# Biases kept in the weights' first row, put there on chip, in place of bias matmuls

## The chip, the cores and the metric

The kernel runs on one core of a Trainium2 chip. A core has five engines that run their own instruction queues and wait for one another by semaphores: PE (TensorE, matmuls; PEld is its weight load), DVE (VectorE), ACT (ScalarE), POOL (GpSimd) and SP (SyncE, which here only issues DMAs). The DMA transfers of all queues run on 16 DMA engines. The metric is the device time of one execution in microseconds, as the median of the runs.

## The reference

One transformer layer over x of 4 x 1024 x 512 in float32: a layernorm, an attention with 16 heads of 128, and a product in rounded fp8 values, added to x.

```python
xn = _layernorm(x)                                  # no scale, no shift
q  = apply_rope(rmsnorm(xn @ Wq + bq, qn_w))        # 16 heads x 128
lk = apply_rope(rmsnorm(xn @ Wlk + blk, kn_w))
lv = xn @ Wlv + blv
w_cmp   = softmax(xn @ Wcmp + bcmp) over each 4 rows
entries = weighted sum of each 4 rows of xn
ck = apply_rope(rmsnorm(entries @ Wk + bk, kn_w));  cv = entries @ Wv + bv
ctx_sparse = softmax over the 8 best (q . ck, causal) @ cv
ctx_local  = softmax over the window of this and the last 128 rows (q . lk) @ lv
out = x + 0.5 * (ctx_sparse + ctx_local) @ Wo + bo + fp8(xn * scale) @ fp8(input2 * scale1) / (scale * scale1)
```

A row of xn has mean zero: its 512 features add up to 0.

## The kernel before

**Tiling.** The 4096 rows are 32 chunks t of 128 rows (8 chunks c of each of 4 batches). The 16 heads are 8 units u of 2 heads, so there are 256 units n = 8t + u. The weights of all units stay in SBUF: wqk_sb[u] (128 x 4 x 512: the columns of Wq and Wlk for the two heads, 4 slices of 128 input features), wlv_sb[u] (128 x 4 x 256) and wo_sb[u].

**Order.** The program is written out by hand in the loop at L789, one step s for each unit, in a software pipeline; each engine runs its instructions in this order. In step s, PE does the scores of unit s (L570 to L581), the queries and keys of unit s + 2 (L443, then a bias matmul L444), the output product of unit s - 2 (L751), the values of unit s + 1 (L535) and the context of unit s - 1 (L718). DVE and ACT do the softmaxes of unit s (weigh, settle, settle_window), then turn (L659) the probabilities of unit s, then normalize and rotate q and lk of unit s + 2 (L465, L308 to L310), with GpSimd for 1/sqrt (L288, L289) and part of the rotation (L307).

**The way through DRAM.** From unit 8 on (by_dma), transposed operands are made in two parts: DVE transposes blocks of 32 x 32 (L659 for the probabilities, L510 and L513 for q and lk), and the blocks change places by a DMA to DRAM and another back. All of them are on SP's queue, in this order in a step: pr out (L667), four probT in (L701), four qk out (L518), qT and lkT in (L528). SP stops at each until the transfer before has landed or the tile is ready. lkT of unit s + 2, made at the end of step s, is read by the scores of that unit (L577).

**Biases.** bq and blk are added by L444: a selection column of sel, spread over 128 columns, times bias_b, which holds the biases split in three bf16 parts (small_constants, L196 to L201). blv is added after the softmax, where the weights of a row add up to 1: keep_context (L733) adds blvT with the factor 0.5, one instruction for each head.

**Work of a chunk.** chunk_prep(t) is a generator, advanced by steps() twice in each step; it begins at u = 7 two chunks ahead and makes layernorm (L327 to L335), the transposed xnT (L340, L343), and the compressed entries. chunk_eight(t), begun at u = 3, rounds xnT to fp8 values (quantize: three DVE passes, four GpSimd passes) and multiplies them with w2_sb (L423). x8 has one buffer. Weights come in by DMA in the first steps: units 0 to 2 on SP's queue, the others on ACT's in steps -2 to 6.

Of the kernel before, what the change touches and what calls it, by code (L numbers as in the profile page):

```python
# [12 lines left out]
F32 = mybir.dt.float32  # L13
BF16 = mybir.dt.bfloat16
U32 = mybir.dt.uint32
AF = mybir.ActivationFunctionType
# [3 lines left out]
P = 128  # L20
# [18 lines left out]
def kernel(  # L39
# [109 lines left out]
    with nc.allow_non_contiguous_dma(reason="512 words once"):  # L149
        nc.scalar.dma_start(  # L150
            wkv_sb[:, :, 2 * D : 2 * D + 1], Wcmp.rearrange("(k p) o -> p k o", p=P)
        )
    bias_f = work.tile([P, 1024], F32, tag="probT", name="bias_f", bufs=1)[0:BLK, 0:512]
    nc.vector.memset(bias_f, 0.0)
    nc.scalar.dma_start(bias_f[0:NU, 0:256], bq.rearrange("(u n) -> u n", u=NU))
    nc.scalar.dma_start(bias_f[0:NU, 256:512], blk.rearrange("(u n) -> u n", u=NU))
    bkv_sb = const.tile([NE, 2 * D], F32, name="bkv_sb")
    nc.scalar.dma_start(bkv_sb[:, 0:D], bk.partition_broadcast(NE))
    nc.scalar.dma_start(bkv_sb[:, D : 2 * D], bv.partition_broadcast(NE))
    norm_w = const.tile([P, 2, D], F32, name="norm_w")  # L160
    nc.scalar.dma_start(norm_w[:, 0, :], qn_w.partition_broadcast(P))
    nc.scalar.dma_start(norm_w[:, 1, :], kn_w.partition_broadcast(P))
    blv_n = work.tile([P, 2, P], F32, tag="cT", name="blv_n", bufs=1)[0:NH, 0, :]
    nc.scalar.dma_start(blv_n, blv.rearrange("(h d) -> h d", h=NH))
    bcmp_sb = const.tile([P, 1], F32, name="bcmp_sb")
    nc.scalar.dma_start(bcmp_sb, bcmp.partition_broadcast(P))
    scales = const.tile([P, 2], F32, name="scales")
# [11 lines left out]
    make_identity(nc, ident)  # L179
    ident_b = const.tile([P, P], BF16, name="ident_b")  # L180
    inv = const.tile([P, 1], F32, name="inv")
    bias_b = const.tile([P, 512], BF16, name="bias_b")
    nc.vector.memset(bias_b, 0.0)
    sel = const.tile([P, NU], BF16, name="sel")
    mask_b = const.tile([P, 2 * P + NE], BF16, name="mask_b")
    bo_sb = const.tile([P, HID], F32, name="bo_sb")
    blvT = const.tile([P, NH], F32, name="blvT")

    def small_constants():
        nc.vector.tensor_scalar(  # L190
            norm_w[:, 0, :], norm_w[:, 0, :], 1.0 / math.sqrt(D), None, ALU.mult
        )

        part = work.tile([P, 1024], F32, tag="probB", name="part", bufs=1).bitcast(BF16)
        part = part[0:BLK, 0:512]
        nc.vector.tensor_copy(bias_b[0:BLK, :], bias_f)  # L196
        nc.vector.tensor_tensor(bias_f, bias_f, bias_b[0:BLK, :], ALU.subtract)
        nc.vector.tensor_copy(part, bias_f)
        nc.vector.tensor_copy(bias_b[BLK : 2 * BLK, :], part)
        nc.vector.tensor_tensor(bias_f, bias_f, part, ALU.subtract)  # L200
        nc.vector.tensor_copy(bias_b[2 * BLK : 3 * BLK, :], bias_f)  # L201

        nc.vector.tensor_tensor(
            sel, ident[:, 0:NU], ident[:, BLK : BLK + NU], ALU.add
        )
        nc.vector.tensor_tensor(
            sel, sel, ident[:, 2 * BLK : 2 * BLK + NU], ALU.add
        )
# [36 lines left out]
    def late_constants():  # L245

        nc.scalar.dma_start(bo_sb, bo.partition_broadcast(P))
        nc.vector.tensor_tensor(inv, scales[:, 0:1], scales[:, 1:2], ALU.mult)
        nc.vector.reciprocal(inv, inv)

        bp = pp("blvT_ps")
        nc.tensor.transpose(bp[:, 0:NH], blv_n, ident[:NH, :NH])
        nc.scalar.activation(blvT, bp[:, 0:NH], AF.Copy, scale=0.5)

    def quantize(dst, src, scalar, tag):

        v = scratch(f"qv_{tag}") if tag[0] == "x" else src
        m = scratch(f"qm_{tag}")  # L260
        nc.vector.tensor_scalar(v, src, scalar, None, ALU.mult)
        nc.vector.tensor_scalar(
            m.bitcast(U32), v.bitcast(U32), 0x7F800000, None, ALU.bitwise_and
        )
        nc.vector.tensor_scalar(m, m, FP8_MIN_NORMAL, 1.5 * 2.0**20, ALU.max, ALU.mult)
        nc.gpsimd.tensor_tensor(v, v, m, ALU.add)
        yield
        nc.gpsimd.tensor_tensor(v, v, m, ALU.subtract)
        yield
        nc.gpsimd.tensor_scalar(m, v, FP8_OVERFLOW, 0.0, ALU.mult, ALU.mult)  # L270
        yield
        nc.gpsimd.tensor_tensor(dst, v, m, ALU.add)
        yield
# [5 lines left out]

    def round_w2():  # L280
        for k in range(KK):
            yield from quantize(w2_sb[:, k, :], w2_raw[k], scales[:, 1:2], f"w2_{k}")

    def rstd_of(ss, n, mul, eps, name):

# [30 lines left out]
    def chunk_prep(t):  # L316
# [14 lines left out]
        if c == 0:  # L331
            nc.gpsimd.memset(cv, 0.0)
        yield "B0"
        xn = scratch(f"xn_{t}")
        nc.vector.tensor_scalar(xn, xt, st[:, 6:7], r, ALU.subtract, ALU.mult)  # L335
        yield "A1"
        yield "B1"
        xp = pp(f"xp_{t}")
# [10 lines left out]
        for k in range(KK):  # L349
# [21 lines left out]
        )  # L371
        nc.scalar.activation(row[:, 0, :], row[:, 0, :], AF.Exp)
        yield "B3"
        yield "A4"
        spread_w = work.tile([P, NE], F32, tag="spread", name=f"spread_{t}", bufs=1)
        nc.vector.transpose(row[:, 1, :], row[:, 0, :])
        nc.vector.tensor_scalar(spread_w, picks, row[:, 1, 0:1], None, ALU.mult)
        yield "B4"
        ep = pp(f"ep_{t}")
        nc.tensor.matmul(ep[0:NE, 0 : 2 * D + 1], spread_w, y, start=True, stop=True)  # L380
        yield "A5"
        total = work.tile([NE, 1], F32, tag="total", name=f"total_{t}", bufs=1)
        kv = work.tile([NE, 2, D], F32, tag="kv", name=f"kv_{t}", bufs=1)
# [6 lines left out]
            ALU.mult,  # L390
            ALU.add,
        )
        yield "B5"
        g, o = divmod(c * NE, P)
        nc.scalar.copy(cv[o : o + NE, g, :], kv[:, 1, :])
# [16 lines left out]
        nc.vector.tensor_copy(ckT[:, ts(c, NE)], cp[:, 0:NE])  # L412
        yield "B8"

    def chunk_eight(t):

        xt, xnT = x_tiles["sum", t], chunks[t]
        x8 = work.tile([P, KK * P], BF16, tag="x8", name=f"x8_{t}", bufs=1)
        src = xnT.rearrange("p k s -> p (k s)")
        yield from quantize(x8, src, scales[:, 0:1], f"x_{t}")  # L420
        fp = pp(f"fp_{t}")
        for k in range(KK):
            nc.tensor.matmul(  # L423
                fp, x8[:, ts(k, P)], w2_sb[:, k, :], start=(k == 0), stop=(k == KK - 1)
            )
        yield
        f = scratch(f"f_{t}")
        nc.vector.scalar_tensor_tensor(f, fp, inv, bo_sb, ALU.mult, ALU.add)
        nc.gpsimd.tensor_tensor(xt, xt, f, ALU.add)
# [4 lines left out]
    def place(n):  # L434

        return divmod(n, NU)

    def queries(n):
        t, u = place(n)
        xnT = chunks[t]  # L440
        qp = psum.tile([P, 512], F32, tag="qp", name=f"qp_{n}")
        for k in range(KK):
            nc.tensor.matmul(qp, xnT[:, k, :], wqk_sb[u][:, k, :], start=(k == 0), stop=False)  # L443
        nc.tensor.matmul(  # L444
            qp, sel[:, u : u + 1].to_broadcast([P, P]), bias_b, start=False, stop=True
        )
        ss = work.tile([P, 4], F32, tag="ss", name=f"ss_{n}")
        units[n] = {"qp": qp, "ss": ss}

# [80 lines left out]
    def values_of(n):  # L530
        t, u = place(n)
        xnT = chunks[t]
        vp = pp(f"vp_{n}")
        for k in range(KK):
            nc.tensor.matmul(  # L535
                vp[:, 0:256],
                xnT[:, k, :],
                wlv_sb[u][:, k, :],
                start=(k == 0),
                stop=(k == KK - 1),  # L540
            )
        units[n]["vp"] = vp

    def keep_values(n):
# [180 lines left out]
        w["cp"] = cp  # L725

    def keep_context(n):
        _, u = place(n)
        w = units[n]
        cT = work.tile([P, 2, P], F32, tag="cT", name=f"cT_{n}", bufs=1)  # L730
        cp = w.pop("cp")
        for h in range(2):
            nc.scalar.activation(  # L733
                cT[:, h, :],
                cp[:, h, :],
                AF.Identity,
                bias=blvT[:, 2 * u + h : 2 * u + h + 1],
                scale=0.5,
            )
        w["cT"] = cT  # L740

    outs = {}
# [46 lines left out]
    for s in range(-2, NN + 2):  # L789
# [3 lines left out]
            running = [*running[-2:], chunk_prep(t + 2)]  # L793
        if u == 3 and 0 <= t < NT:
            load_x(t, "sum")
            running = [*running[-2:], chunk_eight(t)]
        if u == 4 and 0 <= t and t + 2 < NT:
            load_x(t + 2, "norm")
# [32 lines left out]
        if s + 2 >= NU:  # L831
            for_unit(s + 2, (turn_keys,), (fetch_keys,))
        for_unit(s + 1, (keep_values,))
        if s < NU:

            if s == -1:
                late_constants()
                for k in range(KK):
                    nc.scalar.dma_start(w2_raw[k], input2[ts(k, P), :])
            if 0 <= s < KK:  # L840
# [57 lines left out]
```

## Time and profile before

| | us |
|---|---|
| median of 3 runs | 2824.78 |
| lowest, highest | 2822.69, 2830.02 |
| profiled execution | 2828.88 |
| its span in the trace | 2827.2 |
| mean granted PE clock | 0.997 |

In the profile "busy" is the time in which an engine had an instruction running. The ends of matmuls are modelled, and they overlap, so what a matmul costs in a stream is read from the starts of two in a row. "us to landing" of a DMA runs from its issue. A line of the timeline gives start, duration, engine, line, operation and tiles.

```profile
POOL 3433222222233332232223233222223222322222
PEclk9999999999999999999999999999999999999999
HBM read 212.53 MB, written 184.03 MB: 140 GB/s over the span
```

The first two rows are 40 slices of the span, in tenths: POOL is busy 20 to 40% all along, and PE's clock is full throughout.

### The profile page before, as it was taken

How to read it: one execution, taken by the hardware profiler on the slowest of the kernel's cores; microseconds unless marked ns; L12 is line 12 of the kernel's file. 1: busy time of each engine (PE TensorE's matmuls, PEld its weight loads, DVE VectorE, ACT ScalarE, POOL GpSimd, SP SyncE). 2: the span in 40 equal slices, each digit the busy share in tenths (PEclk: the TensorE clock that was granted, in tenths of full speed). 3: DMA queues.
4: the chain of work that ended last, by engine and by line, in shares of the span. 5: the costliest groups of instructions: out<-in, count | busy, mean ns of one | idle time of the engine just before them, and what ended most of it. 6: DMA issues, size and time to landing. Idle time of an engine off the chain costs nothing. (4 is left out here: it accounts for less than half of the span.)

```text
span 2827.2 us, 48528 instructions
## 1 busy us (share of the span) xinstructions
PE 2775.0 (98%) x12770; PEld 1879.6 (66%) x12969; DVE 2277.4 (81%) x9132; ACT 1302.9 (46%) x5075; POOL 818.0 (29%) x1161
## 2 busy tenths in 40 slices
PE   7999999999999999999999999999999999999998
PEld 4666666666666666666666666666666666666666
DVE  5778888888777888888877788888887777888886
ACT  3444444444444444444444444444444444444443
POOL 3433222222233332232223233222223222322222
PEclk9999999999999999999999999999999999999999
DMA  7344445555444445555544444555554444455553
GB/s 224 93 140 133 137 143 151 147 153 146 133 128 133 138 134 149 148 152 151 148 129 123 137 134 138 150 153 147 149 146 124 134 131 131 136 152 151 149 149 116
DMA packets 620851, 399.85 MB, mean 141 GB/s; under 512 B 306880, under 2 KB 573984, under 8 KB 620576
## 3 DMA queue, kind: packets, MB, share of 16 engines
q1 hardware_dynamic: 608352, 383.18, 47.8%
q10 hardware_dynamic: 12224, 13.56, 1.5%
q8 instruction: 105, 1.72, 0.3%
q14 instruction: 170, 1.39, 0.2%
HBM read 212.53 MB, written 184.03 MB: 140 GB/s over the span
## 5 line engine op out<-in xcount | busy, mean ns | idle before, releaser
L443 PE MATMUL qp<-wqk,xnT 128*128 128x512 f32 x2048 | 944.6, 604 | 4.1 <-DMA scales<-in_L_ffn_scale_dram 3.1
L443 PEld LDWEIGHTS qp<-wqk,xnT 128*128 128x128 f32 x2048 | 370.1, 191 | 383.9 <-issue 370.3
L610 ACT ACTIVATE prob<-sc,neg 128x256 f32<-128x256 f32 (+1 forms) x512 | 236.1, 461 | 786.4 <-DVE taken L609 772.5
L535 PEld LDWEIGHTS vp<-wlv,xnT 128*128 128x128 f32 x2048 | 391.1, 191 | 170.4 <-issue 109.5
L535 PE MATMUL vp<-wlv,xnT 128*128 128x256 f32 x2048 | 488.6, 382 | 6.2 <-DVE lkT L495 2.9
L751 PE MATMUL op<-wo,cT 128*128 128x512 f32 x1024 | 488.0, 599 | 6.0 <-ACT cT L733 1.5
L659 DVE STREAM_TRANSPOSE probB<-prob 128x512 f32<-128x512 f32 (+2 forms) x494 | 282.9, 610 | 79.4 <-ACT prob L641 75.8
L294 ACT ACTIVATE junk<-qp 128x128 bf16<-128x128 f32 x1024 | 284.2, 278 | 100.0 <-remote 56.6
L307 POOL TENSOR_TENSOR rb<-th,cs 128x256 f32<-128x256 f32 x256 | 247.4, 966 | 276.5 <-DVE th L465 276.5
L465 DVE SCALAR_TENSOR_TENSOR th<-qp,r,norm_w 128x128 f32<-128x128 f32 x1024 | 282.9, 338 | 45.1 <-POOL r L289 44.9
L751 PEld LDWEIGHTS op<-wo,cT 128*128 128x128 f32 x1024 | 186.5, 190 | 179.2 <-issue 115.9
L547 ACT COPY lv<-vp 128x256 f32<-128x256 f32 x256 | 95.4, 373 | 449.5 <-PE cp L718 393.5
L288 POOL TENSOR_SCALAR r<-ss 128x4 f32<-128x4 f32 x256 | 49.8, 195 | 862.8 <-ACT junk L294 856.4
L718 PE MATMUL cp<-probT,lv 128*128 128x128 f32 x1920 | 298.3, 275 | 0.7 <-DMA probT<-pr 0.7
L718 PEld LDWEIGHTS cp<-probT,lv 128*128 128x128 f32 x1920 | 275.3, 192 | 14.3 <-PE vp L535 1.1
L289 POOL TENSOR_TENSOR r<-r,nhalf 128x4 f32<-128x4 f32 x256 | 259.9, 1015 | 21.4
L718 PE MATMUL cp<-probT,cv 128*128 128x128 f32 x1536 | 255.6, 275 | 0.0
L580 PE MATMUL sc<-ckT,qT 128*128 128x96 f32 (+7 forms) x1024 | 226.2, 303 | 0.0
L641 ACT ACTIVATE prob<-prob,tot 128x256 f32<-128x256 f32 (+1 forms) x512 | 223.0, 484 | 2.1 <-DVE tot L635 2.0
L309 DVE TENSOR_TENSOR th<-thb,rb 128x128 f32<-128x128 f32 x256 | 87.1, 340 | 158.9 <-POOL rb L307 158.9
L577 PE MATMUL sc<-lkT,qT 128*128 128x128 f32 x1024 | 209.7, 287 | 5.4 <-DMA lkT<-qk 3.9
L718 PEld LDWEIGHTS cp<-probT,cv 128*128 128x128 f32 x1536 | 213.2, 192 | 0.0
(123 smaller groups left out, 4003.8 us busy)
## 6 DMA issues: line engine op xcount, KB each, us to landing
pr<-probB SPq DMA_DIRECT2D x127, 512.0 KB, 2.6
probT<-pr SPq DMA_DIRECT2D x508, 128.0 KB, 2.9
qk<-thb SPq DMA_DIRECT2D x992, 64.0 KB, 2.0
pr<-probB SPq DMA_DIRECT2D x96, 384.0 KB, 2.3
probT<-pr SPq DMA_DIRECT2D x384, 96.0 KB, 2.5
qT<-qk SPq DMA_DIRECT2D x248, 128.0 KB, 2.3
lkT<-qk SPq DMA_DIRECT2D x248, 128.0 KB, 2.5
x_norm<-_attn_hidden_states_dram SPq DMA_DIRECT2D x32, 256.0 KB, 3.1
```

The costliest lines, as they stand in the source:

```text
L289: nc.gpsimd.tensor_tensor(r, r, nhalf[: ss.shape[0], 0:n], ALU.pow)
L294: nc.scalar.activation(junk[: src.shape[0]], src, AF.Square, accum_out=acc)
L307: nc.gpsimd.tensor_tensor(bb, x12, wide(cs[:, HALF:ROPE]), ALU.mult)
L443: nc.tensor.matmul(qp, xnT[:, k, :], wqk_sb[u][:, k, :], start=(k == 0), stop=False)
L465: nc.vector.scalar_tensor_tensor(th[:, i, :], qp[:, ts(i, D)], r[:, i : i + 1], norm_w[:, i // 2, :], ALU.mult, ALU.mult,)
L535: nc.tensor.matmul(vp[:, 0:256], xnT[:, k, :], wlv_sb[u][:, k, :], start=(k == 0), stop=(k == KK - 1),)
L580: nc.tensor.matmul(sc[:, spa], q, ckT[:, 0:m], start=True, stop=False)
L610: nc.scalar.activation(prob[:, loc], sc[:, loc], AF.Exp, bias=neg[:, 0:1], scale=-1.0, accum_out=tot[:, 0:1],)
L641: nc.scalar.mul(prob[:, loc], prob[:, loc], tot[:, 0:1])
L659: nc.vector.transpose(pb[:, :, ds(h * g, g), :], prob[:, parts[0] * P : (parts[-1] + 1) * P].rearrange("p (g b i) -> p b g i", b=NB, i=BLK),)
L718: nc.tensor.matmul(blocks(cp[:, h, :]), v, probT[:, :, h * len(parts) + i - parts[0], :], start=(i == parts[0]), stop=(i == parts[-1]),)
L751: nc.tensor.matmul(op, cT[:, h, :], wo_sb[u][:, h, :], start=(u == 0 and h == 0), stop=(u == NU - 1 and h == 1),)
```

## The change

In chunk 0 the biases are added as before by bias matmuls, and blv now likewise, on vp. From chunk 1 on no bias is added at all: xnT's first feature is set to 1.0 and the first row of the weights holds the bias. The feature that this displaces is had from the others: since the features of a row add up to zero, x0 = -(x1 + ... + x511), so the weights' first row w0 is subtracted from all rows, which makes w0 itself 0, and the bias is written in its place. The subtraction is done in SBUF by DMAs that accumulate into the weights (fold_first_row), two for each unit from POOL's queue in steps 3 to 10, from a DRAM row "less" that holds -w0 (first_rows, step -1). One step later put_biases writes the biases by three small DMAs from SP. For the sum to be zero to the last bits, layernorm gets a second centring pass. quantize of chunk t + 2 moves into chunk_prep, since it must read xnT before the first feature is set.

```diff
-    bias_f = work.tile([P, 1024], F32, tag="probT", name="bias_f", bufs=1)[0:BLK, 0:512]
+    bias_f = work.tile([P, 1024], F32, tag="probT", name="bias_f", bufs=1)[0:BLK, 0:768]
...
+    nc.scalar.dma_start(bias_f[0:NU, 512:768], blv.rearrange("(u n) -> u n", u=NU))
...
-    blv_n = work.tile([P, 2, P], F32, tag="cT", name="blv_n", bufs=1)[0:NH, 0, :]
-    nc.scalar.dma_start(blv_n, blv.rearrange("(h d) -> h d", h=NH))
...
-        bp = pp("blvT_ps")
-        nc.tensor.transpose(bp[:, 0:NH], blv_n, ident[:NH, :NH])
-        nc.scalar.activation(blvT, bp[:, 0:NH], AF.Copy, scale=0.5)
...
+    less = dram.tile([NU, 768], F32, name="less", bufs=1)
+
+    def first_rows():
+        row = work.tile([P, 1024], F32, tag="probT", name="first_rows", bufs=1)[0:NU, 0:768]
+        for i, w in enumerate((Wq, Wlk, Wlv)):
+            nc.sync.dma_start(row[:, ts(i, 256)], w[0].rearrange("(u n) -> u n", u=NU))
+        nc.gpsimd.tensor_scalar(row, row, -1.0, None, ALU.mult)
+        nc.gpsimd.dma_start(less, row)
+
+    def fold_first_row(u):
+        for w, cols in ((wqk_sb[u], ds(0, 512)), (wlv_sb[u], ds(512, 256))):
+            row = less[u, cols].partition_broadcast(P).unsqueeze(1)
+            nc.gpsimd.dma_start(w, row.to_broadcast([P, KK, w.shape[2]]), accum_op=ALU.add)
+
+    def put_biases(u):
+        for w, at, bias in ((wqk_sb[u], 0, bq), (wqk_sb[u], 256, blk), (wlv_sb[u], 0, blv)):
+            nc.sync.dma_start(w[0:1, 0, ds(at, 256)], bias[ts(u, 256)].partition_broadcast(1))
...
-        nc.vector.tensor_scalar(xn, xt, st[:, 6:7], r, ALU.subtract, ALU.mult)
+        off = work.tile([P, 1], F32, tag="off", name=f"off_{t}")
+        nc.vector.tensor_scalar(xn, xt, st[:, 6:7], 0.0, ALU.subtract, ALU.add, accum_out=off)
+        nc.vector.tensor_scalar(off, off, 1.0 / HID, None, ALU.mult)
+        nc.vector.tensor_scalar(xn, xn, off, r, ALU.subtract, ALU.mult)
...
         yield "B3"
+        if t:
+            eights[t], step = begin_eight(t)
+            next(step)
+            nc.vector.memset(xnT[0:1, 0, :], 1.0)
         yield "A4"
...
+    def begin_eight(t):
+        x8 = work.tile([P, KK * P], BF16, tag="x8", name=f"x8_{t}")
+        src = chunks[t].rearrange("p k s -> p (k s)")
+        return x8, quantize(x8, src, scales[:, 0:1], f"x_{t}")
...
+    def add_biases(out_, u, cols):
+        nc.tensor.matmul(
+            out_, sel[:, u : u + 1].to_broadcast([P, P]), bias_b[:, cols], start=False, stop=True
+        )
...
-        nc.tensor.matmul(
-            qp, sel[:, u : u + 1].to_broadcast([P, P]), bias_b, start=False, stop=True
-        )
+        if not t:
+            add_biases(qp, u, ds(0, 512))
...
+        if not t:
+            add_biases(vp[:, 0:256], u, ds(512, 256))
...
-        for h in range(2):
-            nc.scalar.activation(
-                cT[:, h, :],
-                cp[:, h, :],
-                AF.Identity,
-                bias=blvT[:, 2 * u + h : 2 * u + h + 1],
-                scale=0.5,
-            )
+        nc.scalar.activation(cT, w.pop("cp"), AF.Copy, scale=0.5)
...
+        if u == (5 if t else 4) and 0 <= t < NT:
             running = [*running[-2:], chunk_eight(t)]
...
         for_unit(s + 1, (keep_values,))
+
+        if 0 <= s - 3 < NU:
+            fold_first_row(s - 3)
+        if 0 <= s - 4 < NU:
+            put_biases(s - 4)
```

The other three steps of the moved quantize are advanced at the three next places of chunk_prep; chunk_eight then begins at u = 5 with the product. The scratch of quantize for the second weight comes from a part of wo_sb that is not loaded yet.

More of the change, by code (lines that the diff above doesn't have):

```diff
@@ L181 @@
     inv = const.tile([P, 1], F32, name="inv")
-    bias_b = const.tile([P, 512], BF16, name="bias_b")
+    bias_b = const.tile([P, 768], BF16, name="bias_b")
     nc.vector.memset(bias_b, 0.0)
@@ L186 @@
     bo_sb = const.tile([P, HID], F32, name="bo_sb")
-    blvT = const.tile([P, NH], F32, name="blvT")
     def small_constants():
@@ L194, in small_constants @@
         part = work.tile([P, 1024], F32, tag="probB", name="part", bufs=1).bitcast(BF16)
-        part = part[0:BLK, 0:512]
+        part = part[0:BLK, 0:768]
         nc.vector.tensor_copy(bias_b[0:BLK, :], bias_f)
@@ L249, in late_constants, with quantize @@
         nc.vector.reciprocal(inv, inv)
-        bp = pp("blvT_ps")
-        nc.tensor.transpose(bp[:, 0:NH], blv_n, ident[:NH, :NH])
-        nc.scalar.activation(blvT, bp[:, 0:NH], AF.Copy, scale=0.5)
-    def quantize(dst, src, scalar, tag):
+    less = dram.tile([NU, 768], F32, name="less", bufs=1)
[12 more added lines that the diff above has]
+            nc.sync.dma_start(w[0:1, 0, ds(at, 256)], bias[ts(u, 256)].partition_broadcast(1))
+    def quantize(dst, src, scalar, tag, m=None):
         v = scratch(f"qv_{tag}") if tag[0] == "x" else src
-        m = scratch(f"qm_{tag}")
+        if m is None:
+            m = scratch(f"qm_{tag}")
         nc.vector.tensor_scalar(v, src, scalar, None, ALU.mult)
@@ L281, in round_w2 @@
         for k in range(KK):
-            yield from quantize(w2_sb[:, k, :], w2_raw[k], scales[:, 1:2], f"w2_{k}")
+            spare = wo_sb[NU // 2 + k][:, 1, :]
+            yield from quantize(w2_sb[:, k, :], w2_raw[k], scales[:, 1:2], f"w2_{k}", spare)
     def rstd_of(ss, n, mul, eps, name):
@@ L377, in chunk_prep @@
         nc.vector.tensor_scalar(spread_w, picks, row[:, 1, 0:1], None, ALU.mult)
+        if t:
+            next(step, None)
         yield "B4"
@@ L380, in chunk_prep @@
         nc.tensor.matmul(ep[0:NE, 0 : 2 * D + 1], spread_w, y, start=True, stop=True)
+        if t:
+            next(step, None)
         yield "A5"
@@ L392, in chunk_prep @@
         )
+        if t:
+            next(step, None)
         yield "B5"
@@ L413, in chunk_prep @@
         yield "B8"
+    eights = {}
+    def begin_eight(t):
+        x8 = work.tile([P, KK * P], BF16, tag="x8", name=f"x8_{t}")
+        src = chunks[t].rearrange("p k s -> p (k s)")
+        return x8, quantize(x8, src, scales[:, 0:1], f"x_{t}")
     def chunk_eight(t):
[L417 to L420, printed above, removed]
+        if not t:
+            eights[t], step = begin_eight(t)
+            yield from step
+        x8 = eights.pop(t)
         fp = pp(f"fp_{t}")
@@ L426, in chunk_eight @@
         yield
+        xt = x_tiles["sum", t]
         f = scratch(f"f_{t}")
@@ L442, in queries @@
         for k in range(KK):
-            nc.tensor.matmul(qp, xnT[:, k, :], wqk_sb[u][:, k, :], start=(k == 0), stop=False)
-        nc.tensor.matmul(
-            qp, sel[:, u : u + 1].to_broadcast([P, P]), bias_b, start=False, stop=True
-        )
+            nc.tensor.matmul(
+                qp,
+                xnT[:, k, :],
+                wqk_sb[u][:, k, :],
+                start=(k == 0),
+                stop=(t > 0 and k == KK - 1),
+            )
+        if not t:
+            add_biases(qp, u, ds(0, 512))
         ss = work.tile([P, 4], F32, tag="ss", name=f"ss_{n}")
@@ L539, in values_of @@
                 start=(k == 0),
-                stop=(k == KK - 1),
+                stop=(t > 0 and k == KK - 1),
             )
+        if not t:
+            add_biases(vp[:, 0:256], u, ds(512, 256))
         units[n]["vp"] = vp
@@ L727, in keep_context @@
     def keep_context(n):
-        _, u = place(n)
         w = units[n]
         cT = work.tile([P, 2, P], F32, tag="cT", name=f"cT_{n}", bufs=1)
-        cp = w.pop("cp")
-        for h in range(2):
-            nc.scalar.activation(
-                cT[:, h, :],
-                cp[:, h, :],
-                AF.Identity,
-                bias=blvT[:, 2 * u + h : 2 * u + h + 1],
-                scale=0.5,
-            )
+        nc.scalar.activation(cT, w.pop("cp"), AF.Copy, scale=0.5)
         w["cT"] = cT
@@ L839 @@
                     nc.scalar.dma_start(w2_raw[k], input2[ts(k, P), :])
+            if s == -1:
+                first_rows()
             if 0 <= s < KK:
```

## The prediction

> **What bounds the kernel now.** I read the engine shares of the page first, then who TensorE waited for, then two stretches of the timeline (one steady step, one step's end in detail), then the DMA rows, and the early DMA load by window.
>
> ```profile
> PE 2775.0 (98%) x12770; PEld 1879.6 (66%) x12969; DVE 2277.4 (81%) x9132; ACT 1302.9 (46%) x5075; POOL 818.0 (29%) x1161
> ```
> ```profile
> PE sc L577 <- DMA lkT<-qk: 3.9, 8, 1.2
> PE sc L570 <- DMA qT<-qk: 2.0, 3, 1.4
> ```
>
> PE is busy 98% of the span, and the waits listed for it come to 34 us, 21 of them in the first 110 us. In the steady part the only repeated wait is for the keys that come back from DRAM (lkT, qT): 11 times in 248 units, 5.9 us. So PE's instruction stream sets the end, and the keys' path is the runner-up. What one bias matmul costs is seen in start times, since ends of matmuls are modelled:
>
> ```profile
> 1431.03 3.68 PE L443 MATMUL qp<-wqk,xnT 128*128 128x512 f32 x8
> 1434.55 0.38 PE L444 MATMUL qp<-bias_b,sel 128*128 128x512 bf16 x1
> 1434.77 1.88 PE L751 MATMUL op<-wo,cT 128*128 128x512 f32 x4
> ```
>
> From L444's start to L751's start 0.22 us pass (where its record is missing, the gap after the last L443 is longer by 0.216). The keys' path, for the unit whose scores start at 1418.82:
>
> ```profile
> 1406.54 0.34 SPq L667 DMA_DIRECT2D pr<-probB  x1
> ...
> 1409.13 0.45 DVE L510 STREAM_TRANSPOSE thb<-th 128x256 f32<-128x256 f32 x1
> 1409.21 1.75 SPq L701 DMA_DIRECT2D probT<-pr  x4
> 1409.50 0.40 DVE L513 STREAM_TRANSPOSE thb<-th 128x256 f32<-128x256 f32 x1
> ...
> 1411.00 1.89 SPq L518 DMA_DIRECT2D qk<-thb  x4
> ...
> 1414.70 1.03 SPq L528 DMA_DIRECT2D lkT<-qk  x1
> ...
> 1419.06 0.40 PE L577 MATMUL sc<-lkT,qT 128*128 128x128 f32 x2
> ```
> ```profile
> qk<-thb SPq DMA_DIRECT2D x992, 64.0 KB, 2.0
> lkT<-qk SPq DMA_DIRECT2D x248, 128.0 KB, 2.5
> bo_sb<-in_L_attn_bo_dram ACTq DMA_DIRECT2D x1, 256.0 KB, 4.5
> ```
>
> The reader is to see a chain through one queue: SP sends pr, waits, issues four probT, then four qk, waits, then qT and lkT. lkT is issued at 1414.70, lands 2.5 later at 1417.2, and is read at 1419.06: 1.9 us to spare. Pairing issues, landings and readers for all 248 such units I get a median of 1.2 us to spare, a quarter under 0.66, 31 units under 0.30, 44 under 0.45. That is all the room the rest of the pipeline has. The early DMA load, in 40 slices of 2.75 us (0 to 110 us), and by window (span, PE, PEld, DVE, ACT, POOL busy, clock, DMA share, GB/s):
>
> ```profile
> DMA  2993889999331899559605970992005501600050
> GB/s 60 242 267 92 228 258 369 345 351 352 111 95 61 293 327 366 204 196 328 238 0 163 340 258 9 307 356 98 6 0 166 216 0 5 188 0 0 6 191 0
> ```
> ```profile
> 100.00:120.00 20.00, 19.82 (x91) 12.94 (x92) 13.70 (x68) 8.64 (x39) 5.43 (x8) 1.00 0.24 67
> 120.00:140.00 20.00, 19.95 (x94) 13.41 (x94) 14.29 (x66) 10.10 (x43) 5.06 (x8) 1.00 0.36 95
> 140.00:160.00 20.00, 19.89 (x98) 14.34 (x99) 15.35 (x69) 8.89 (x33) 4.20 (x6) 1.00 0.49 142
> ```
>
> Plain weight loads fill the DMA engines (a 9) at about 350 GB/s; from 100 to 160 us, where the new traffic goes, the engines are already 0.24 to 0.49 busy.
>
> [...]
>
> **The change part by part.**
> Bias matmuls: 248 of 256 L444 go (chunks 1 to 31, 8 units each): 248 x 0.216 = 53.6 us, all on PE's path. The next matmul (L751 and the rest) keeps its 0.43 pace since its loads ran beside L444 and now run beside the last L443. Added: eight 256-column bias matmuls on vp in chunk 0, half of 0.216 each, 0.9 us; the transpose L252 goes, 0.2 us. PE net: -52.9.
>
> Keys' path: the chain from qp(n)'s end to scores(n) has one foreign bias matmul inside it, and where DVE and not qp starts the chain, two. Room shrinks by 0.22 to 0.43 in every unit. The 44 units with less than 0.45 lose at most 0.43 each, 19 us, at the least half of 0.22 in 31 units, 3; I take 12 given back as new waits for lkT and qT.
>
> Layernorm: L335 (542 ns) becomes a centring pass with a sum, a one-column scaling and a second pass: 542 + 83 (accumulator read as at L625) + 154 (one column as at L608) more, plus a one-row memset of some 85 ns (L176): 0.86 us of DVE per chunk, 28 us over 32 chunks. DVE is 81% busy and its order behind this is L659, then the keys of one unit per chunk, so it eats room only there. 0.86 against a median 1.2 less 0.3: mostly hidden; I take 0.1 per chunk, 3 us, and 0.86 x 32 = 28 if the room is gone.
>
> keep_context: two L733 (367 ns each) become one 128x256 copy, nearest L547 at 373: 0.36 us of ACT per unit. ACT is 46% busy and cT is ready 4.9 us before L751 reads it (1408.73 against 1413.59): nothing.
>
> The quantize steps move from chunk_eight(t) into chunk_prep(t+2), at the same places of a step (three DVE passes at u = 3, GpSimd's four after them), with x8 doubled: nothing. At the start bias_f grows from 512 to 768 columns (six DVE passes, 2.9 us, half more: 1.4 us, ahead of L361, which DVE waited 6.4 for): nothing. first_rows puts three loads on SP and a scaling and a DMA on GpSimd ahead of the first probT: hidden behind the wait for the loads of the first 60 us.
>
> The fold: in steps 3 to 10 GpSimd issues 1.05 + 0.52 = 1.57 MB of accumulating DMA per step. [...] That its source is one row read over and over is no extra: bo_sb, the same kind of read, lands in 4.5 us beside 256 KB loads at 4.2. Each step is 10.3 us long, so 0.87 + 0.24 to 0.49 is over one from step 6 on. By the step ends in the timeline the first is issued near 83.5 us: 72 us of folds + about 33 us of other traffic (0.36 x 91) end near 188, where SP comes to the last put at about 174: 14 us late. Who waits: put_biases stands in SP's queue behind the fold it completes and ahead of pr, probT and qk of the next step, and its landing is waited for by queries two steps on (from the timeline about 0.5 us spare). Slower landings of qk, pr and lkT in the shared rings in five steps, about 1 us each beyond the room: 5 us. Three puts per step on SP, 0.4 us each, fit the 1.35 us that SP waits for probB before a pr (296.7 us in 219 waits). Sum 19 us. [...] From above 70, see the rivals. Descriptors: GpSimd has 7.2 us free from L307's end (1408.57) to its next work (1415.76); under that, nothing, and what is over delays r by as much in eight steps.
>
> Sum: -52.9 + 12 + 3 + 19 = -18.9. The profiled execution took 2828.88 (span 2827.2 and 1.7 around it), 4.1 above the median of 2824.78; the same difference on the median gives **2806**.
>
> **Rivals.**
> Everything hides: the fold fits (5), the keys hold (3): -45, 2780. For it: the median room of 1.2 us; against: engines already 0.49 busy.
> The keys' path takes over: room is short in all units once DVE has 28 us more and PE runs ahead, so that most of the 53.6 returns as waits on lkT: about -5, 2820. For it: the thin room; against: only 11 waits now.
> Slower: the fold's DMA is slow. If it takes 18 us of engines per step and not 9, the step is 18 + 4 long, about 11 more for eight steps, 88 less the 14 us of head start: 74. -52.9 + 15 + 74 = +36, 2861. It decides from a cost of 36 us, which is about 11 us per fold; for it: nothing in this trace has run such a DMA[...]; against: the copies' 350 GB/s.
>
> **How the numbers follow.** Forecast 0.40, everything hides 0.18, keys take over 0.13, slower 0.29. What a measurement of this kernel tells from no change is about 0.3%, 8.5 us. Faster: 0.18 + 0.37 of the forecast's 0.40 (its own range is 2790 to 2822) = 0.55; same: 0.03 + 0.12 = 0.15; slower: 0.30 with the rest. The range is from 2776 (everything hides) to 2858 (most of the slow fold).
>
> **What would show it.** L444 with 8 matmuls and the step shorter by 0.22 us from 200 us on; PE's waits for lkT and qT grown from 5.9 to some 18 us; a stretch of 85 to 190 us that is longer than before by some 19, with DMA share near 1 and SP waiting for the folds. I am wrong if that stretch is longer by over 36 us, or if PE's waits after 200 us exceed 40.

## The result, and the profile after

| us | before | after |
|---|---|---|
| median | 2825.97 (4 runs) | 2852.54 (4 runs) |
| lowest, highest | 2822.69, 2830.02 | 2851.49, 2853.60 |
| profiled execution | 2828.88 | 2852.95 |
| its span | 2827.2 | 2850.5 |

The ratio is 1.0094 (95% interval 1.0078 to 1.0110): the kernel became slower by 26.6 us, where 19 us less had been forecast. The page of the kernel after (engine shares, the granted clock in 40 slices, one DMA queue), and then, from its view of what PE waited for (total us, times, longest):

```profile
PE 2760.9 (97%) x12728; PEld 1867.4 (66%) x12728; DVE 2304.3 (81%) x9259; ACT 1227.3 (43%) x4818; POOL 839.8 (29%) x1179
...
PEclk9979999999999999999999999999999999999999
...
q0 software_dynamic: 8480, 12.61, 2.8%
```
```profile
PE sc L621 <- DMA qT<-qk: 37.2, 14, 14.4
PE sc L628 <- DMA lkT<-qk: 7.8, 18, 0.9
PE vp L584 <- DVE lkT L544: 7.4, 3, 3.3
PE cp L769 <- DMA probT<-pr: 7.1, 2, 4.2
```

PE does 14 us less work and still ends 23 us later in the trace: it waits, and the longest wait is 14.4 us for a single transfer. The third slice of the clock, which read 9 before, reads 7. Both are in one place. The start of each unit's scores, after less before, in us (255 is the last unit):

```
unit      0    6    7     8     9    10    11    12    13    20   248   255
later   0.4  4.6  8.8  23.2  26.8  42.5  45.4  53.8  56.9  55.4  28.6  25.2
```

Everything is lost by unit 13, whose scores start at 232 us: 8.8 us by unit 7, and 48.1 from there to unit 13, in which each unit's keys come through DRAM. From unit 20 on the kernel after is the faster one and gains back 28 us by unit 254. So two questions have separate answers: why the gain is 28 and not 53, and where the 57 us go before it.

**The steady part.** The step around the end of qp, in the timeline of PE after (start, duration, engine, line, tiles):

```profile
1458.62 2.74 PE L487 MATMUL qp<-wqk,xnT 128*128 128x512 f32 x6
1461.19 1.88 PE L793 MATMUL op<-wo,cT 128*128 128x512 f32 x4
```

The bias matmul between the two is gone, and the next product starts 2.57 us after the first of the six matmuls shown, 0.43 for each: no gap is left where it stood. Over units 20 to 254 the starts behind qp come some 49 us earlier in sum, 0.21 for each. In the same units PE's stops in front of and among the scores grow by some 21 us.

**The stretch.** Windows of 5 us of the kernel after (window, length, then PE, PEld, DVE, ACT and POOL busy with their instructions, granted clock, DMA share, GB/s; packets overlap, so the share can pass 1):

```profile
130.00:135.00 5.00, 1.92 (x15) 1.63 (x13) 1.13 (x5) 0.93 (x3) 3.76 (x4) 1.00 0.89 172
135.00:140.00 5.00, 0.00 (x0) 0.00 (x0) 1.93 (x6) 0.00 (x0) 0.28 (x1) 0.65 1.07 161
140.00:145.00 5.00, 0.00 (x0) 0.00 (x0) 0.00 (x0) 0.00 (x0) 0.00 (x0) 0.50 1.11 171
145.00:150.00 5.00, 3.39 (x15) 3.12 (x16) 1.14 (x7) 0.18 (x1) 0.00 (x0) 0.50 0.42 93
150.00:155.00 5.00, 5.00 (x8) 2.14 (x9) 3.93 (x20) 1.35 (x6) 0.00 (x0) 0.64 0.23 53
155.00:160.00 5.00, 5.00 (x26) 3.68 (x25) 2.55 (x7) 2.94 (x12) 1.60 (x3) 1.00 0.14 54
```

From 140 to 145 us no engine does anything, while the DMA share is 1.11: the core waits for transfers alone. At 155 they are all through, the DMA share is 0.14, and PE is full. Then it begins again: in 175 to 185 us PE does nothing either. What the transfers are is read from two queues of the same timeline. GpSimd's folds, and then SP's:

```profile
119.08 1.33 POOL L264 DMA_DIRECT2D wqk<-less  x1
119.93 1.80 POOL L264 DMA_DIRECT2D wlv<-less  x1
...
132.63 1.32 POOL L264 DMA_DIRECT2D wqk<-less  x1
133.48 1.79 POOL L264 DMA_DIRECT2D wlv<-less  x1
```
```profile
124.28 2.24 SPq L567 DMA_DIRECT2D qk<-thb  x4
135.02 0.38 SPq L577 DMA_DIRECT2D qT<-qk  x1
135.45 1.42 SPq L577 DMA_DIRECT2D lkT<-qk  x1
```
```profile
131.53 0.39 PE L769 MATMUL cp<-probT,cv 128*128 128x128 f32 x2
146.36 0.77 PE L621 MATMUL sc<-lkT,qT 128*128 128x128 f32 x2 [14.44 <-DMA qT<-qk]
...
149.74 5.58 PE L487 MATMUL qp<-wqk,xnT 128*128 128x512 f32 x8
155.16 1.88 PE L793 MATMUL op<-wo,cT 128*128 128x512 f32 x4
...
160.94 3.68 PE L487 MATMUL qp<-wqk,xnT 128*128 128x512 f32 x8
```

The four qk are issued by 126.5 and qT, which waits for them alone, goes out at 135.0: 8.5 us, with a fold of 119.9 still under way until about then (it lands 15.2 us after its issue, at 135.1; the median of the eight wlv folds is 14.6), and for part of it a 512 KB load on ACT's queue. That is one. qT then meets the next fold, of 132.63 and 133.48, and PE gets it at 146.36, 11.3 us after its issue (that wlv fold lands 13.4 after its own, at 146.9). That is two, in series, for one unit's keys.

The packets in the trace tell the second wait in two parts (queue, packets, MB, share of 16 engines; q0 is GpSimd's queue, q1 SP's). First from 135 to 140.5 us, in which qT and lkT are already issued, then from 140.5 to 144:

```profile
q0 software_dynamic: 427, 0.87, 106.8%
```
```profile
q0 software_dynamic: 451, 0.52, 92.1%
q1 hardware_dynamic: 351, 0.09, 19.8%
```

In the first part only the fold's packets run. SP's first one comes at 140.7, 5.7 us after the issue of qT, where 1.0 us passes in the kernel without folds (experiment 1) and some 1.0 in the kernel before (from 129.7 to 130.7). What holds it back is not shown. In the second part the two queues move packets at like rates, but those of SP hold about 256 bytes and the fold's over 1 KB, so that SP gets a seventh of the bytes.

PE's waits between the scores of units 7 and 13 (122 to 232 us) add up to 36.2 us, all of them for transfers: 28.4 in three for qT, 7.1 in two for probT, 0.7 in two for lkT. In experiment 1 PE has no such wait in these units.

The rest of the 48.1 is mostly clock. The last three lines of PE's timeline above show part of it: the same eight matmuls of qp take 5.58 us after the wait and 3.68 one unit later. In the windows above, the granted clock is 1.00 in 130 to 135, where PE stops, 0.65 in the next one, 0.50 from 140 to 150, 0.64 in 150 to 155, where PE is busy again, and 1.00 from 155. Around the stop of 175 to 185 it is 0.50 until 190, 0.89 in 190 to 195 and 1.00 from 195. From the first scores to the start of what follows qp, the three stalls for qT (146.36, 185.59 and 218.54) took 8.8, 8.1 and 8.4 us against 5.0 for unit 9: 3.8, 3.1 and 3.4 more, 0.7 of it the waits for lkT. The two contexts behind a wait for probT (171.41 and 212.94) took 2.9 instead of 1.3. Together, without the 0.7, that is some 13 us. 36 and 13 are 49, and six bias matmuls less take 1.3 off: the 48.1 are accounted for.

### The profile page after: what moved, and what is told of

It reads as the page before. It is cut to its first block, busy times and chain, and to the rows that moved or that the text cites. A ratio compares the mean times of both kernels' runs of the same rounds, so it can differ in the third digit from the quotient of the medians.

```text
span 2850.5 us, 48135 instructions
## 1 busy us (share of the span) xinstructions
PE 2760.9 (97%) x12728; PEld 1867.4 (66%) x12728; DVE 2304.3 (81%) x9259; ACT 1227.3 (43%) x4818; POOL 839.8 (29%) x1179
## 5 line engine op out<-in xcount | busy, mean ns | idle before, releaser
L621 PE MATMUL sc<-lkT,qT 128*128 128x128 f32 x896 | 200.6, 306 | 38.7 <-DMA qT<-qk 37.2
L654 DVE CUSTOM_DVE_ANT_0 sc<-sc,mask_b 128x256 f32<-128x256 f32 (+1 forms) x512 | 202.5, 396 | 28.1 <-PE sc L632 28.1
L628 PE MATMUL sc<-lkT,qT 128*128 128x128 f32 x1024 | 214.2, 291 | 9.6 <-DMA lkT<-qk 7.8
```

The costliest lines, as they stand in the source:

```text
L628: nc.tensor.matmul(blocks(sc[:, P : 2 * P]), q, lkT[:, :, ds(h * BLK, BLK)], start=True, stop=True)
```

## The experiments

Four theories stood at the start, A to D in the expectations. A: the loss is the folds' transfers, which hold up whatever SP moves beside them. B: it is in what the change adds in every chunk and unit (second layernorm pass, moved work, thinner room for the keys). C: it is the puts, behind which SP stands. D: it is GpSimd's own work at the issue of the folds (1.3 and 1.8 us in its timeline above). Later theories ask where the gain of the missing bias matmuls goes: to SP's own issuing, which sets the keys' round trip (F), or to another pace (E); in experiments 6 and 7, A is that it goes into waits for qT and lkT. Ratios are to the kernel before on the same chip, with 95% intervals.

**1. No folds.** From the kernel after, first_rows, fold_first_row and put_biases are taken out.

```diff
-        if 0 <= s - 3 < NU:
-            fold_first_row(s - 3)
-        if 0 <= s - 4 < NU:
-            put_biases(s - 4)
...
-            if s == -1:
-                first_rows()
```

> The changed kernel without first_rows, fold_first_row and put_biases: all else stays, so from chunk 1 on no bias is added and the first feature is lost (left out: the biases of chunks 1 to 31). Theory A (all of the loss lies in the fold's stretch, 85 to 210 us,[...]): the 58 us that units 4 to 13 lost come back whole, the clock there is near 1.0, and the time is about 2852 - 58 = 2794. Theory B (the second centring pass and the fuller step cost more than the trace shows, and the fold is only a part): above 2805.

Measured 2810.01 us, 0.9933 (0.9920 to 0.9945). The stretch is whole again: unit 13 starts 3.1 us later than before instead of 56.9, and the clock is 1.00 from 100 us on. Between this run and the kernel after lie 0.0161 of 2826, 45 us, which are the folds' and the puts'. (At unit 13 the two traces are 53.8 us apart, at unit 255 48; why some of it comes back later is not shown.) But 2810 is above the 2788 that the prediction's own terms give without a fold (-52.9 + 12 + 3), so something of B is real as well. SP's timeline and DMA row in this kernel, for comparison with 8.5 and 11.3 above:

```profile
119.65 1.85 SPq L567 DMA_DIRECT2D qk<-thb  x4
123.31 0.38 SPq L577 DMA_DIRECT2D qT<-qk  x1
```
```profile
qk<-thb SPq DMA_DIRECT2D x36, 64.0 KB, 1.8
...
qT<-qk SPq DMA_DIRECT2D x9, 128.0 KB, 2.2
```

**2. The bias matmuls alone.** From the kernel before, L444 is left out from chunk 1 on, and nothing else is changed; q and lk have no bias there.

```diff
-            nc.tensor.matmul(qp, xnT[:, k, :], wqk_sb[u][:, k, :], start=(k == 0), stop=False)
-        nc.tensor.matmul(
+            nc.tensor.matmul(
+                qp, xnT[:, k, :], wqk_sb[u][:, k, :], start=(k == 0), stop=(t > 0 and k == KK - 1)
+            )
+        if not t:
+            nc.tensor.matmul(
```

> The kernel before with nothing changed but L444 left out in chunks 1 to 31 (left out: bq and blk of those chunks). It measures the gain of the bias matmuls alone: 53.6 us on PE's path less what comes back as waits for qT and lkT. If those waits grow only because PE runs faster, it lands with the kernel without folds, within 4 us, near 2794. If the second centring pass and the moved work eat the keys' room, it is faster than that one by 8 us or more, 2785.

Measured 2798.76 us, 0.9893 (0.9880 to 0.9907): 29.9 us for 53.6 us of matmuls. So 24 us come back with the matmuls alone. PE's waits in this kernel, from 220 to 2780 us, where the kernel before has 3.9 us in 8 for lkT and 0.5 in 2 for qT:

```profile
PE sc L580 <- DMA lkT<-qk: 8.8, 16, 1.5
PE sc L573 <- DMA qT<-qk: 8.1, 12, 1.4
PE sc L580 <- ACT cT L736: 2.8, 4, 0.9
PE cp L721 <- DMA probT<-pr: 1.5, 1, 1.5
```

The keys were read on time in nearly all units before and are late 28 times now. The list does not hold all of it (stops too short to be listed are missing): measured by starts, the stops in front of and among the scores grow by some 19 us here too, in units 20 to 254.

**3. Folds without puts.** The kernel after without put_biases: the waits of SP behind the folds go, and the folds stay. The biases are left out.

```diff
-        if 0 <= s - 4 < NU:
-            put_biases(s - 4)
```

> The changed kernel with the folds as they are but without put_biases, so that nothing on SP waits for a fold (left out: the biases of chunks 1 to 31). Theory A (round trips of pr, qk, qT and lkT are slow[...]): 2846 to 2853, hardly less than the changed kernel. Theory C (SP stands behind a put and starts the transfers late): 40 us less, near 2812.

Measured 2858.8 us, 1.0100 (1.0084 to 1.0115), and again 53 and 55 us late at units 12 and 13. SP's queue behind the puts, which took 14 us of the forecast, is not what costs. In the kernel after SP does stand at a put for 63 us, but that is before it has any key to move.

**4. Folds as copies.** The same bytes to the same places, without the add: the weights of chunks 1 on become the first rows.

```diff
-            nc.gpsimd.dma_start(w, row.to_broadcast([P, KK, w.shape[2]]), accum_op=ALU.add)
+            nc.gpsimd.dma_start(w, row.to_broadcast([P, KK, w.shape[2]]))
```

> The changed kernel with the same sixteen DMAs from GpSimd as plain copies of the row over the weights, not accumulating (the weights from chunk 1 on are then that row). [...] Theory A (engine time of the packets): the folds' share of the engines falls by about half, from 79 us to about 42, and half of the 58 us come back: near 2824. Theory D (GpSimd's own work of describing, or its order): unchanged, 2850.

Measured 2850.14 us, 1.0078 (1.0064 to 1.0091), with the same stall: 47.4 us late at unit 13. That is where D stood. A's number, half of the loss back, rested on a copy of half the price, the author's estimate, and this copy is hardly cheaper, so this run does not tell A from D. The rows of DMA issues (KB each, us to landing) and of GpSimd's queue, first after, from 60 to 215 us, then this kernel, from 80 to 210:

```profile
q0 software_dynamic: 8443, 12.58, 50.9%
...
wqk<-less POOLq DMA_DIRECT2D x8, 1024.0 KB, 11.5
wlv<-less POOLq DMA_DIRECT2D x8, 512.0 KB, 14.6
```
```profile
q0 software_dynamic: 3328, 12.58, 50.9%
...
wqk<-less POOLq DMA_DIRECT2D x8, 1024.0 KB, 9.0
wlv<-less POOLq DMA_DIRECT2D x8, 512.0 KB, 12.4
```

50.9% of 155 us is 79 us of all 16 engines for the eight folds with the add, and 50.9% of 130 us is 66 us without: 9.9 and 8.3 us for each. The add is a sixth of the price. The copy of these 12.58 MB runs at 190 GB/s, where the weight loads of the kernel before ran at about 350. Whether that is the one source row or the queue that it is issued on was not tried.

**5. Folds with nobody waiting.** If A holds, the folds may stay as slow as they are, provided that no key has to pass them. The first six units of chunk 1 get their transposed keys and probabilities from PE, as chunk 0 does, and the way through DRAM begins at unit 14.

```diff
+    KD = NU + 6
...
-        return NU <= n < NN - 1
+        return KD <= n < NN - 1
...
-        if not by_dma(s + 1) and s < NU:
+        if s + 1 < KD:
             for_unit(s + 1, (turn_keys_here,))
...
-        if not by_dma(s + 1) and s < NU:
+        if s + 1 < KD:
             for_unit(s + 1, (keep_keys,))
...
+        wide = NU <= s < KD
+        if not by_dma(s) and not wide:
             for_unit(s, (turn_here,))
...
         for_unit(s - 1, (values,))
+        if wide:
+            for_unit(s + 1, (keep_values,))
+            for_unit(s, (turn_here,))
...
-        if s + 2 >= NU:
+        if s + 2 >= KD:
             for_unit(s + 2, (turn_keys,), (fetch_keys,))
-        for_unit(s + 1, (keep_values,))
+        if not wide:
+            for_unit(s + 1, (keep_values,))
```

> The changed kernel, with all folds and puts, but the first six units of chunk 1 have their keys and probabilities turned by PE as in chunk 0, so that no round trip through DRAM stands on SP while the folds run. Theory A (a round trip behind a fold lands only when the fold does, about 10 us instead of 2): the loss of 58 us shrinks to the transposes' own PE time, 6 units x 10 x 0.11 = 7 us, and what PE waits for them, up to 8: 2852 - 58 + 7 to 15 = 2801 to 2809. Theory D (GpSimd's queue is held): at least 30 of the 58 stay, 2825 or more.

Measured 2811.88 us, 0.9955 (0.9941 to 0.9968). Its DMA rows from 80 to 210 us, and three windows:

```profile
wqk<-less POOLq DMA_DIRECT2D x8, 1024.0 KB, 10.5
wlv<-less POOLq DMA_DIRECT2D x8, 512.0 KB, 13.7
```
```profile
120.00:140.00 20.00, 20.00 (x99) 13.61 (x98) 12.35 (x61) 9.56 (x40) 8.11 (x11) 1.00 1.02 167
140.00:160.00 20.00, 20.00 (x109) 14.49 (x108) 13.28 (x62) 9.37 (x36) 8.47 (x9) 1.00 1.03 163
160.00:180.00 20.00, 20.00 (x109) 14.88 (x108) 13.46 (x57) 8.42 (x32) 10.15 (x12) 1.00 0.84 137
```

The folds take nearly as long as they did, the DMA engines are full to about 160 us, and PE is full as well at full clock. 0.9955 against 1.0094 is 39 us: all but some 6 of the 45 are back, with more work on PE. The time is 3 us above A's range and 13 below D's. This decides for A: GpSimd issues the same folds, and it is not the folds' own length that costs, it is who has to pass them.

**6 and 7. The keys ahead of the probabilities.** What sets the room of the keys in the steady part? SP's order in a step is pr, probT, qk, qT and lkT. In experiment 6 (from experiment 2) and 7 (from the kernel before) the qk of unit s + 2 are issued ahead of probT.

```diff
         if by_dma(s):
+            for_unit(s + 2, (turn_keys,))
             fetch(s)
+            for_unit(s + 2, (fetch_keys,))
         else:
             for_unit(s, (keep_turned,))
-        if s + 2 >= NU:
-            for_unit(s + 2, (turn_keys,), (fetch_keys,))
+            if s + 2 >= NU:
+                for_unit(s + 2, (turn_keys,), (fetch_keys,))
```

> The kernel before without L444 in chunks 1 to 31 (left out: bq and blk of those chunks), and with qk issued ahead of the four probT on SP, so that qT and lkT go out about 1 us earlier and probT 1.9 us later (which had 3 to 4 us to spare). Theory A (the 20 us that do not show of the 50.5 saved after unit 20 are waits for qT and lkT): at least 12 of them come back, 2786 or less. Theory E (they are another wait or DVE's pace): within 4 us of the 2798.8 without that reordering.

> The kernel before with qk ahead of probT and nothing else. PE waited only 5.9 us for qT and lkT there, so theory A gives 3 to 6 us, near 2822; theory E nothing.

Measured 2806.75 us, 0.9929 (0.9915 to 0.9942), and 2837.75 us, 1.0044 (1.0032 to 1.0057): each slower than what it was made from. PE's waits of experiment 6, from 220 to 2780 us:

```profile
PE cp L721 <- DMA probT<-pr: 25.8, 35, 2.1
PE sc L580 <- DMA lkT<-qk: 3.4, 4, 1.6
```

The wait has changed places. The keys are on time, and the probabilities are late in 35 units. The two have no room to lend each other.

**8. One layernorm pass.** Experiment 1 with the second pass taken out.

```diff
-        off = work.tile([P, 1], F32, tag="off", name=f"off_{t}")
-        nc.vector.tensor_scalar(xn, xt, st[:, 6:7], 0.0, ALU.subtract, ALU.add, accum_out=off)
-        nc.vector.tensor_scalar(off, off, 1.0 / HID, None, ALU.mult)
-        nc.vector.tensor_scalar(xn, xn, off, r, ALU.subtract, ALU.mult)
+        nc.vector.tensor_scalar(xn, xt, st[:, 6:7], r, ALU.subtract, ALU.mult)
```

> The changed kernel without folds and puts, and with the one-pass layernorm of before (left out: biases of chunks 1 to 31, and the exact zero mean). Against the same kernel with both passes (2810.0): if the 11 us by which that one is slower than the kernel before without L444 are the second pass on DVE, about 2800; if they come from the moved rounding, the memset or chunk 0, no change, 2810.

Measured 2798.23 us, 0.9903 (0.9890 to 0.9917). Against experiment 1 this is 0.0030 of 2826, 8.5 us for the pass, with some 5 us of uncertainty from the two intervals. It lies where experiment 2 lies (0.9893), which has none of the other parts: the moved rounding, the memset of the first feature, keep_context in one instruction and chunk 0's biases on vp cost 3 us with some 5 of uncertainty, so nothing that the times can tell. The traces do show a cost in chunk 0: at unit 7 this kernel is 5.9 us later than before and experiment 2 0.3 us earlier. Up to 130 us its PE waits 9.9 us for DVE's copy of the keys that PE turned (keep_keys), 2.9 in the kernel before. By unit 255 the two are 2.5 us apart.

**9 and 12. The qk on two queues.** F: SP issues four qk at about 0.45 us each and then waits. Two of the four go to ACT's queue, behind keep_values. Experiment 9 starts from experiment 2, experiment 12 from the kernel before.

```diff
-            nc.sync.dma_start(
+            (nc.scalar if a < 2 else nc.sync).dma_start(
                 turned[a].rearrange("b j x -> j b x"),
...
+        for_unit(s + 1, (keep_values,))
         if s + 2 >= NU:
             for_unit(s + 2, (turn_keys,), (fetch_keys,))
-        for_unit(s + 1, (keep_values,))
```

> The kernel before without L444 in chunks 1 to 31 (left out: bq and blk of those chunks), with two of the four qk of a unit issued from ACT's queue, so that SP's serial round of a step is about 0.9 us shorter. Theory F (with the bias matmuls gone, the serial round of DMA issues and landings on SP is a second limit beside PE; putting qk first only moved the wait from qT and lkT to probT): the waits for qT and lkT fall without new ones for probT, 2785 to 2792 against 2798.8. Theory E (another pace, DVE's or ACT's, holds it): 2797 to 2802, or slower if ACT's queue now stands behind thb.

> The kernel before with half of each qk on ACT's queue. PE waited only 5.9 us for qT and lkT there: theory F gives at most 6 us, 2820 to 2826; theory E 2825 or slower.

Measured 2805.06 us, 0.9927 (0.9915 to 0.9939), and 2838.73 us, 1.0043 (1.0030 to 1.0056): slower both times. SP's waits for qk from 220 to 2780 us, in experiment 2 and then in experiment 9:

```profile
SPq L531 <- DMA qk<-thb: 323.7, 325, 2.0
```
```profile
SPq L531 <- DMA qk<-thb: 415.5, 326, 4.0
...
SPq L521 <- DMA qk<-thb: 141.8, 89, 3.2
```

ACT issues its two at once (median 0.03 us after the blocks are turned), but SP still issues its own two only 1.27 us after, behind probT, and is then through with them sooner, so that it waits longer for their landing. qT goes out 4.35 us after the blocks are turned instead of 4.56: 0.2 us are won. In experiment 9 PE also waits 5.9 us in seven units for cT, which ACT now makes behind its two issues. F in this form is not supported; all four on ACT's queue were not tried, and what makes the kernels slower beyond that is not shown.

**10 and 11. The best of these.** Experiment 5 with the one-pass layernorm of experiment 8, and the same with the qk on two queues; the edits are those of experiments 5, 8 and 9.

> The changed kernel with the first six units of chunk 1 turned by PE, and with the one-pass layernorm of before. The second pass cost 8 to 11 us where the folds were left out; the same here: 2801 to 2804 against 2811.9. If its cost was tied to the missing folds, 2810 to 2813.

> As the one before, with half of each qk on ACT's queue. Theory F: 8 to 14 us faster than it, 2788 to 2796. Theory E: no faster.

Measured 2805.55 us, 0.9922 (0.9910 to 0.9934), and 2808.39 us, 0.9935 (0.9922 to 0.9947). The first is the fastest that has all of the change's parts but the second pass: 21 us faster than the kernel before, 47 faster than the kernel after. Between experiments 5 and 10 lie 0.0033 of 2826, 9.3 us for the second pass, as in experiment 8. The mean of a row is then zero only as far as one pass makes it.

## Why the prediction was wrong

The direction was wrong: faster was forecast, by 18.9 us, and it is slower by 26.6. The terms of the sum, with what the runs give for each. The measured ones are a chain of differences between runs, so their sum has to meet the result; each is uncertain by some 5 us:

| term | predicted | measured | from |
|---|---|---|---|
| PE net | -52.9 | -52.9 | taken as forecast; 0.21 us for each in the starts behind qp |
| keys' path | +12 | +24 | experiment 2: 53.6 less 29.9 |
| second layernorm pass | +3 | +9 | experiments 1 and 8 |
| moved work and start | 0 | +2 | experiments 8 and 2, less 0.7 that is in PE net |
| fold | +19 | +45 | after less experiment 1 |
| sum | -18.9 | +27 | +26.6 measured |

**Bias matmuls.** Right to the step: 0.21 for each, and the next product fills the place without a gap.

**Moved quantize, keep_context, the start.** Costed at nothing. Experiment 8 beside 2 shows nothing beyond its uncertainty, but the start was not free: some 6 us are lost in chunk 0 by unit 7, with waits for keep_keys that were not in the forecast.

**Keys' path.** Right in kind, wrong in size, and outside its bounds of 3 to 19. The waits for qT and lkT were forecast to grow from 5.9 to some 18 us; from 220 us on, behind the stretch, they list 15.6. But what comes back is twice the 12. The term was sized from the room in the profile of before, with only the 44 units below 0.45 us paying and each paying once. In experiment 2 the stops grow by some 19 us, although the change took at most 0.43 from any unit's room. A likely reason, argued and not shown, is that the room was itself made by PE's being slow: once PE runs ahead, the next units start with less. Room measured as in the prediction, on the 187 units whose landing the trace has, agrees: its median is 0.84 us in experiment 2 instead of 1.2, and 62 units instead of 32 lie below 0.45.

**Second pass.** Its instructions, from the groups of DVE after (busy us, mean ns at the end):

```profile
L354 DVE TENSOR_SCALAR_CACHE_REDUCE xn<-x_norm,lnst 128x512 f32<-128x512 f32 x32 | 23.7, 740 | 0.0
L356 DVE TENSOR_SCALAR xn<-xn,off,lnr 128x512 f32<-128x512 f32 x32 | 17.5, 546 | 1.2
```

With 84 ns for the reading of the accumulator and 154 for the scaling, that is 0.98 us more than the 0.54 of before, where 0.78 was forecast for these three (the memset, forecast at 0.085, took 0.165). The cover was overrated: 0.1 us per chunk was taken as seen, and 8.5 / 32 = 0.27 was.

**Fold.** This is the step that failed. Three things in it came out near to what was put. The engine time: 9.0 us per fold forecast, the author's estimate (0.87 of a step, 72 us for eight), 9.9 measured. That was luck: 1.57 MB at the 350 GB/s of the weight loads would be 4.5 us, but a plain copy is 8.3, and the add takes 1.6 more. So what bo_sb showed, "no extra" for a source of one row, does not price this DMA as a whole. The add runs here at 159 GB/s and the copy at 190. GpSimd's own time at the issue of a fold, 1.3 and 1.8 us, lies in the gap where it was put. And the DMA engines are full, as the sum of shares said: 0.89 to 1.11 in 130 to 145 us.

What failed is the term of 5 us for slower landings of qk, pr and lkT in five steps, "about 1 us each beyond the room". The fold's price was reckoned as capacity: bytes over rate, and a queue that ends 14 us late. What small transfers lose beside it was put at 1 us a step without a reason. In place of it, a transfer of 64 or 128 KB, issued on another queue beside a fold, landed 8.5 and 11.3 us after its issue instead of 1.8 and 2.2, about when the fold did (qk by 135.0 and qT by 146.4, the folds at 135.1 and 146.9). A unit's operands need two or more such transfers one after the other (pr and probT, qk and qT), so a unit can pay twice. That made 36 us of PE waits in the stretch, and the lower clock behind them (0.50 granted from 140 to 150 us) some 13 more. Experiment 5 shows it from the other side: the same folds cost some 6 us of the 45 when no such transfer is due.

The 14 us of the fold's other term (SP late at the last put) were not seen: experiment 3 has no puts and the same loss. The rival "slow fold" had named the right place and the right sign, with "the fold's DMA is slow" as mechanism and 11 us per fold as its point. The fold took less than that and the loss came anyway, since it is the latency of the transfers beside it that decides and not only the engines' time.

**The signs named beforehand.** Of the two that would show the forecast wrong, the stretch did (57 us longer, over the 36), and PE's waits after 200 us did not (28.5 us are listed, against 40).

**What stays open.** What sets the round of pr, probT, qk, qT and lkT in the steady part: its order on SP can't be turned without a new wait (6, 7), and two queues brought qT out only 0.2 us earlier (9). What keeps SP's packets from starting for some 5 us beside a fold. Also why the copy runs at 190 GB/s.

## What to carry to other kernels

Price a large transfer by the transfers that must pass it, and not only by its bytes: for each small transfer issued beside it ask how late the reader can take it, and count the transfers in series. If they can't wait, keep the large one out of that stretch, or keep the small ones off the DMA there (here 39 us). Work taken from the engine that sets the end counts in full only as far as the next path has room, and the room that a profile shows was measured with the slower engine: here 30 of 53.6 us remained.

## What was not expected of the hardware

- Small transfers did not pass a large one in their own time here, although it is on another queue: qk took 8.5 us instead of 1.8 beside a fold of 1.57 MB. From 140.5 to 144 us packets of both queues run, 351 of SP's and 451 of the fold's, with 0.09 MB against 0.52. In the 5.5 us before, no packet of SP's queue ran, although qT and lkT were issued on it, at 135.0 and 135.5; why is not shown.
- A wait of PE cost more than its length: after one of 14.4 us, at whose end 0.50 of the clock was granted, the next scores and queries took 8.8 us instead of 5.0.
- An add in the DMA cost 20% over the copy of the same bytes (79 against 66 us of all engines), and moved in 2.5 times the packets (8443 against 3328).
